# In the edge network of a graph kernel, the beginning of a chunk is put ahead of the network of the chunk in front of it

## The chip, the core and the metric

The kernel runs on one core of a Trainium2 chip. The time is the device time of one execution in microseconds (us), as the median of several runs. The profile is one further execution, recorded by the hardware profiler. The engines are named as in the profile: PE is TensorE (PEld its weight loads), DVE is VectorE, ACT is ScalarE, POOL is GpSimd and SP is SyncE. SP, ACT and POOL also issue DMAs; the gathers and scatters of single rows are all issued by POOL.

## What is computed

Four graph layers run one after the other over 6250 nodes of 48 features and 200000 edges, sorted by their end `dst`. The change touches the second layer only, a network on each edge whose results are averaged at the edge's end node:

```python
def _L1_gnn_ref(x, edge_index, edge_feat, W1, b1, W2, b2, W3, b3):
    source = edge_index[0]
    target = edge_index[1]
    edge = jnp.concatenate([x[source], x[target], edge_feat], axis=-1)   # 48 + 48 + 16
    h = jax.nn.relu(edge @ W1 + b1)                                       # 112 -> 128
    h = jax.nn.relu(h @ W2 + b2)                                          # 128 -> 128
    message = h @ W3 + b3                                                 # 128 -> 48
    msum = jax.ops.segment_sum(message, target, num_segments=n)
    cnt = jax.ops.segment_sum(jnp.ones(...), target, num_segments=n)
    return x + msum / jnp.maximum(cnt, 1.0)[:, None]
...
x = _layernorm(x + _L0_gnn_ref(...), axis=-1)
x = _layernorm(x + _L1_gnn_ref(x, edge_index, edge_attr_16, ...), axis=-1)
x = _layernorm(x + _L2_gnn_ref(x, edge_index, edge_weight), axis=-1)
x = _layernorm(x + _L3_gnn_ref(x, edge_index, 6250), axis=-1)
```

All matrices are 32-bit floats.

## The kernel before

Each of the 128 partitions holds a run of 1564 consecutive edges in sorted order, one edge per column. A loop over 41 chunks of columns (38 of 40 columns, then 24, 12 and 8) does the second layer in `edge_mlp`, lines 1172 to 1234. For one chunk `c` of the loop the program says, in this order:

- SP loads `r` (the edge's two ends, its weight and its 16 features, line 1181) and `q` (line 1183). In `q` a node's row stands only at the first edge of that node; elsewhere it is zero.
- `segments_chunk` (lines 801 to 803, DVE) writes the chunk's part of `other`, the indices for the gathers, and of `ns`, which is 1 where an edge has the same end as the one before it. ACT copies the weights into `dw` (line 1185).
- POOL gathers the row of the edge's other end from `tab_x` in device memory, one indirect DMA for each column (line 1188; in the profile line 166, the helper). They fill the first 48 of 112 numbers of an edge in the tile `t`.
- The rows of `q` are spread over the edges of a node by a scan along the columns (`runs`, lines 257 to 270). Four times, for 12 features each, ACT copies a part into PSUM (`run_v`, line 286), DVE adds what comes from the chunk before (line 267) and scans into `qf` (line 269). ACT copies `qf` into the next 48 numbers of `t` (line 1193) and the features from `r` into the last 16 (line 1194).
- The network goes over the chunk in turns of four columns: PE transposes four columns of `t` (line 1200), ACT copies them to `at` (1202), PE does the first layer (1207), ACT its relu to `h1` (1209), PE the second layer (1214), DVE its relu to `h2` (1216), PE the third layer (1222), and DVE copies the result to `msg` (1223). `skewed` puts the four stages of neighbouring turns side by side, so that turn i's transposes stand by turn i-1's first layer and so on.
- The messages are summed along the columns by another `runs` into `sf` (line 1227), copied to `st` by ACT (line 1230) and stored to `state_h` (line 1231). Later stages pick a node's sum out at its last edge.

The buffers come from pools: two of each tile in `ep` unless the call names another number. `qf`, `sf`, `msg` and `st` have one, `t`, `r`, `q`, `at`, `h1` and `h2` two. In PSUM the transposes, the first two layers together and the scans' `run_v` have two buffers each, and the third layer has one. A tile's buffer is free for the next tile of its name when the last reader of the old one is done. A planner puts every engine's instructions into one list, starting from the program's order but not bound to it; each engine then runs its list strictly in order, and waits where an instruction's operands or its buffer are not ready. So in the list of before a few small steps of later chunks, such as `other` and `ns`, already stand inside a chunk's network, while the scan of `q` and the copy into `t` stand behind the chunk before.

Of the kernel before, what the change touches and what calls it, by code (L numbers as in the profile page):

```python
# [20 lines left out]
N, E, H = 6250, 200000, 48  # L21
# [5 lines left out]
CHUNKS = [(i * C, C) for i in range(38)] + [(1520, 24), (1544, 12), (1556, 8)]  # L27
# [9 lines left out]
def pj(t):  # L37
    return t.rearrange("(p j) w -> p j w", j=J)
# [7 lines left out]
def gnn_kernel(ctx: ExitStack, tc: tile.TileContext, A, out: bass.AP):  # L46
    nc = tc.nc
    V, S, T = nc.vector, nc.scalar, nc.tensor
# [26 lines left out]
    before = const.tile([P, P], F32, name="before")  # L75
# [87 lines left out]
    tab_x = dram.tile([NP, H], F32, name="tab_x")  # L163

    def gather(dst, table, idx):
        return nc.gpsimd.indirect_dma_start(  # L166
            out=dst, out_offset=None, in_=table, in_offset=bass.IndirectOffsetOnAxis(ap=idx, axis=0))
# [37 lines left out]
    def by_columns(pool, wid, w, name, cols=C, **kw):  # L205

        return pool.tile([P, cols, w], F32, name=name, **kw)[:, :wid, :]

    def by_features(pool, w, wid, name, cols=C, **kw):

        t = pool.tile([P, w, cols], F32, name=name, **kw)
        return t.rearrange("p f c -> p (f c)")[:, :w * wid].rearrange("p (f c) -> p f c", c=wid)
# [28 lines left out]
    def factors(pool, name, fg=FG, cols=C):  # L241

        ts = [pool.tile([P, fg, cols], F32, name=f"{name}{i}", bufs=1) for i in range(2)]
        for t in ts:
            V.memset(t, 0.0)

        def put(c, v):
            wid = v.shape[1]
            t = ts[c % 2].rearrange("p f c -> p (f c)")[:, :fg * wid]
            u = t.rearrange("p (f c) -> p f c", c=wid)  # L250
            if wid < cols:
                V.memset(u[:, :, 0:1], 0.0)
            S.copy(u[:, :, 1:], v[:, None, 1:].to_broadcast([P, fg, wid - 1]))
            return t
        return put

    def runs(psum, dst, fac, first, before_, w, put, fg=FG, cols=C):


        wid = dst.shape[2]  # L260
        flat = dst.rearrange("p f c -> p (f c)")
        for f0 in range(0, w, fg):
            n = min(fg, w - f0)
            v = by_features(psum, fg, wid, "run_v", cols)
            put(v[:, :n, :], f0, n)
            if before_ is not None:
                V.scalar_tensor_tensor(v[:, :n, 0], before_[:, f0:f0 + n], first, v[:, :n, 0],  # L267
                                       op0=OP.mult, op1=OP.add)
            V.tensor_tensor_scan(flat[:, f0 * wid:(f0 + n) * wid], fac[:, :n * wid],  # L269
                                 v.rearrange("p f c -> p (f c)")[:, :n * wid], 0.0, OP.mult, OP.add)  # L270

    def kept_last(pool, t, name):

        k = pool.tile([P, t.shape[1]], F32, name=name)
        V.tensor_copy(k, t[:, :, t.shape[2] - 1])  # L275
        return k

    def by_feature(t):
        return t.rearrange("p c f -> p f c")

    def by_column(t):
        return t.rearrange("p f c -> p c f")

    def copied(src):

        return lambda v, f0, n: S.copy(v, by_feature(src[:, :, f0:f0 + n]))  # L286
# [504 lines left out]
    def segments_begin(k, pool):  # L791
        prev = pool.tile([P, 1], F32, name="seg_prev", bufs=1)
        V.memset(prev, -1.0)
        nc.sync.dma_start(prev[1:P, :], pj(rows[k][:])[0:P - 1, J - 1, 0:1])
        f = pool.tile([P, 1], F32, name="seg_first", bufs=1)
        nc.sync.dma_start(f, pj(rows[k][:])[:, 0, 0:1])
        V.tensor_copy(seg0, f)
        return prev, f

    def segments_chunk(j0, wid, r, prev):  # L800
        V.tensor_copy(other[:, j0:j0 + wid], r[:, :, 1])
        V.tensor_tensor(ns[:, j0:j0 + 1], r[:, 0, 0:1], prev, op=OP.is_equal)
        V.tensor_tensor(ns[:, j0 + 1:j0 + wid], r[:, 1:, 0], r[:, 0:wid - 1, 0], op=OP.is_equal)
        return r[:, wid - 1, 0:1]
# [23 lines left out]
    def skewed(n, *stages):  # L828

        kept = {}  # L830
        for i in range(n + len(stages) - 1):
            for k, stage in enumerate(stages):
                if 0 <= i - k < n:
                    kept[i - k] = stage(i - k, kept.get(i - k))
# [45 lines left out]
    def first_rows(pool, table, name):  # L880
        t = pool.tile([P, H], F32, name=name, bufs=1)
        gather(t, table[:], seg0[:, 0:1])
        return t
# [109 lines left out]
    with tc.tile_pool(name="e0", bufs=2) as ep:  # L993
        with tc.tile_pool(name="e0_ps", bufs=2, space=PSUM) as psum:
            f, last, sums = gated_sums(ep, psum)
# [176 lines left out]
    def edge_mlp(ep, psum, psum1, psum2):  # L1172
        W = 2 * H + EF
        prev, f = segments_begin("d", ep)
        factor = factors(ep, "fac")
        before_q = first_rows(ep, tab_x, "first")
        before_s = None
        for c, (c0, wid) in enumerate(CHUNKS):
            s = slice(c0, c0 + wid)
            r = by_columns(ep, wid, WD, "r")  # L1180
            nc.sync.dma_start(r, pj(rows["d"][:])[:, s, :])
            q = by_columns(ep, wid, H, "q")
            nc.sync.dma_start(q, pj(spread["d"][0:EP, :])[:, s, :])
            prev = segments_chunk(c0, wid, r, prev)
            S.copy(dw[:, s], r[:, :, 2])
            t = by_columns(ep, wid, W, "t")
            for j in range(wid):
                gather(t[:, j, 0:H], tab_x[:], other[:, c0 + j:c0 + j + 1])
            fac, first = factor(c, ns[:, s]), ns[:, c0:c0 + 1]
            qf = by_features(ep, H, wid, "qf", bufs=1)  # L1190
            runs(psum2, qf, fac, first, before_q, H, copied(q))
            before_q = kept_last(ep, qf, "last_q")
            S.copy(t[:, :, H:2 * H], by_column(qf))
            S.copy(t[:, :, 2 * H:], r[:, :, 3:])
            msg = by_columns(ep, wid, H, "msg", bufs=1)

            def turn(i, _):
                ps = psum.tile([W, 4, P], F32, name="ps_t")
                for k in range(4):
                    T.transpose(ps[:, k, :], t[:, 4 * i + k, :], ident)  # L1200
                at = ep.tile([W, 4, P], F32, name="at")
                S.copy(at, ps)
                return at

            def first_layer(i, at):
                ps = psum.tile([HID, 4, P], F32, name="ps_1")
                T.matmul(ps, w1, at, start=True, stop=True)  # L1207
                h1 = ep.tile([HID, 4, P], F32, name="h1")
                S.activation(h1, ps, AF.Relu, bias=b1)  # L1209
                return h1  # L1210

            def second_layer(i, h1):
                ps = psum.tile([HID, 4, P], F32, name="ps_1")
                T.matmul(ps, w2, h1, start=True, stop=True)  # L1214
                h2 = ep.tile([HID, 4, P], F32, name="h2")
                V.tensor_scalar(h2, ps, b2, 0.0, op0=OP.add, op1=OP.max)  # L1216
                return h2

            def third_layer(i, h2):
                ps = psum1.tile([P, 4, H], F32, name="ps_3")  # L1220
                for k in range(4):
                    T.matmul(ps[:, k, :], h2[:, k, :], w3, start=True, stop=True)  # L1222
                V.tensor_copy(msg[:, 4 * i:4 * i + 4, :], ps)

            skewed(wid // 4, turn, first_layer, second_layer, third_layer)
            sf = by_features(ep, H, wid, "sf", bufs=1)
            runs(psum2, sf, fac, first, before_s, H, copied(msg))
            before_s = kept_last(ep, sf, "last_s")
            st = by_columns(ep, wid, H, "st", bufs=1)
            S.copy(st, by_column(sf))  # L1230
            nc.scalar.dma_start(pj(state_h[0:EP, :])[:, s, :], st)
        lastf = ep.tile([P, 1], F32, name="lastf", bufs=1)
        V.tensor_copy(lastf, prev)
        return f, lastf, before_s

    with tc.tile_pool(name="e9", bufs=2) as ep:
        with tc.tile_pool(name="e9_ps", bufs=2, space=PSUM) as psum, \
                tc.tile_pool(name="e9_ps1", bufs=1, space=PSUM) as psum1, \
                tc.tile_pool(name="e9_ps2", bufs=2, space=PSUM) as psum2:
            f, lastf, sums = edge_mlp(ep, psum, psum1, psum2)  # L1240
        with tc.tile_pool(name="e9_ps3", bufs=1, space=PSUM) as psum:
            segments_end("d", ep, psum, f, lastf)
            carries(ep, psum, sums, H, 0)
# [112 lines left out]
```

## Time and profile before

| what | us |
|---|---|
| median of three runs | 21866.9 |
| lowest and highest of them | 21861.03, 21871.99 |
| the profiled execution | 21773.17 |
| its span, from the first to the last instruction | 21771.4 |
| busy: POOL, DVE, PE, ACT | 13854.5, 8090.9, 5782.7, 4790.3 |
| first gather of the second layer from `tab_x` (start) | 14080.9 |
| the second layer's last store, issued by ACT | 17144.5 |
| one gather from `tab_x`, busy, median | 0.944 |
| one copy of a whole chunk (`t<-qf` or `st<-sf`) | 3.917 |
| one `at` copy, one `h1`, one `h2`, one `msg` copy | 0.585, 0.688, 0.751, 0.358 |
| one scan of 480 columns, one `run_v` copy | 1.153, 0.97 |

The page gives one row for each group of instructions: line, engine, operation, output and inputs, how often, busy time and mean duration, and the idle time of the engine just before them with what ended most of it. A line can be that of a helper: all gathers have line 166 and all scans line 269. A timeline gives start, duration, engine, line and operation in order of time, with the idle time before the instruction in brackets and what ended it. In the trace the end of a matmul is modelled, and a few records of matmuls are missing. One matmul of 32-bit floats of the first or second layer shows as two records, so a turn has 16 of them: four transposes, two and two for the first layers, eight for the third.

### The profile page before, as it was taken

To read this page: it belongs to the slowest core of one execution; us is meant where nothing else is said; L and a number is where in the kernel's file an instruction comes from. 1 tells how busy PE (TensorE), PEld (TensorE's weight loads), DVE (VectorE), ACT (ScalarE), POOL (GpSimd) and SP (SyncE) were. 2 spreads that over 40 slices of the span, in tenths; PEclk is the share of its full clock that TensorE was granted. 3 is DMA by queue.
4 is the path that set the end of the run, shared out by engine and by line. 5 is a ranking of instruction groups with operands and counts; after the bars stand their busy time and mean duration, and the time that the engine had idled before them with its cause. 6 is when DMAs were issued, how large, how long until landed. Compare 5 with 4: busy or idle time off the path is not lost.

```text
span 21771.4 us, 87599 instructions
## 1 busy us (share of the span) xinstructions
PE 5782.7 (27%) x19726; PEld 3494.4 (16%) x19726; DVE 8090.9 (37%) x16421; ACT 4790.3 (22%) x6563; POOL 13854.5 (64%) x13410
## 2 busy tenths in 40 slices
PE   2332346622223222322223222245545200000000
PEld 2332334410002000200002000133333100000000
DVE  6554557644333344334333334322222211111001
ACT  0332334411111111111111111133333200001111
POOL 2666641177775777577775777644444577777777
PEclk9999995555555555555555555566666655555555
DMA  5455544332222222222222222211111111111111
GB/s 157 165 172 134 172 169 180 151 87 88 86 83 66 86 87 88 60 89 88 86 81 70 86 85 88 57 40 43 43 46 44 33 36 34 36 36 36 36 36 36
DMA packets 873560, 1792.36 MB, mean 82 GB/s; under 512 B 365490, under 2 KB 546658, under 8 KB 868034
## 3 DMA queue, kind: packets, MB, share of 16 engines
q1 hardware_dynamic: 349038, 860.63, 12.0%
q0 software_dynamic: 427520, 547.67, 10.8%
q10 hardware_dynamic: 96468, 378.32, 4.6%
q8 instruction: 167, 2.74, 0.1%
q14 instruction: 367, 3.01, 0.0%
HBM read 1144.48 MB, written 641.17 MB: 82 GB/s over the span
## 4 chain that ended last, share of the span: by engine, by line
POOL 43%; issue 21%; DVE 10%; another core or an unknown queue 10%; PE 9%; ACT 6%; DMA 1%; ACTq 0%; SPq 0%; POOLq 0%; DVEq 0%
POOL t L166 41%; PE ps L1207 2%; PE ps L1214 2%; PE ps L1222 1%; ACT run_v L286 1%; POOL own L166 1%; DVE qf L269 1%; DVE ol L303 1%; PE g L386 1%; DVE sf L986 1%; PE ps_t L1200 1%; ACT st L1230 1%; ACT st L989 1%; DVE run_v L267 1%
## 5 line engine op out<-in xcount | busy, mean ns | idle before, releaser
L166 POOL DMA_INDIRECT t<-tab_kv,other x6256 | 6576.9, 1051 | 2112.8 <-issue 2069.6
L166 POOL DMA_INDIRECT t<-tab_x,other x4692 | 4788.3, 1021 | 2605.8 <-issue 1457.2
L1124 PE MATMUL ka<-t,ident 128*128 128x480 f32 (+2 forms) x1264 | 1213.3, 1063 | 6798.6 <-DMA t<-tab_kv,other 6015.1
L1126 DVE TENSOR_TENSOR q<-qf,ka 128x480 f32<-128x480 f32 (+2 forms) x632 | 677.9, 1074 | 4126.9 <-issue 3358.9
L171 POOL DMA_INDIRECT rows_s<-r_s,scratch x1564 | 1527.9, 977 | 967.8 <-ACT r_s L421 466.7
L1124 PEld LDWEIGHTS ka<-t,ident 128*128 128x128 f32 x1264 | 316.3, 310 | 7520.9 <-issue 4273.1
L269 DVE TENSOR_TENSOR_SCAN qf<-fac,run_v 128x480 f32<-128x480 f32 (+1 forms) x943 | 1028.8, 1092 | 654.0 <-DVE run_v L267 409.8
L841 PE MATMUL cy_ps<-ident,last_s 128*48 128x128 f32 (+1 forms) x4 | 1.6, 406 | 4523.5 <-DVE last_s L275 4523.5
L1156 ACT COPY st<-m 128x40 f32<-128x40 f32 (+3 forms) x164 | 42.8, 261 | 5233.9 <-DVE sc L1129 4099.3
L386 PE MATMUL g<-hs,olt 128*128 128x49 f32 x3128 | 759.0, 418 | 1231.1 <-ACT hs L384 860.3
L286 ACT COPY run_v<-q 128x480 f32<-128x480 f32 (+1 forms) x943 | 851.7, 916 | 503.1 <-DVE qf L269 197.8
L1125 PE MATMUL ka<-r,tenth 128*128 128x400 f32 (+2 forms) x1264 | 959.7, 863 | 0.0
L1216 DVE TENSOR_SCALAR h<-ps,b 128x512 f32<-128x512 f32 x391 | 293.6, 751 | 1725.5 <-PE ps L1207 829.7
L386 PEld LDWEIGHTS g<-hs,olt 128*128 128x128 f32 x3128 | 696.1, 327 | 1283.6 <-ACT hs L384 893.0
L1304 DVE TENSOR_TENSOR run_v<-t,w_ps 128x480 f32<-128x480 f32 (+3 forms) x164 | 142.1, 912 | 1832.6 <-DMA t<-tab_x,other 1832.6
L267 DVE SCALAR_TENSOR_TENSOR run_v<-last_s,ns,run_v 128x12 f32<-128x12 f32 x480 | 98.0, 219 | 1934.1 <-issue 1280.6
L924 POOL TENSOR_TENSOR r<-r,u 128x1920 f32<-128x1920 f32 (+3 forms) x41 | 135.5, 3305 | 1034.3 <-DVE u L923 931.1
L269 DVE TENSOR_TENSOR_SCAN sf<-dec,run_v 128x480 f32<-128x480 f32 (+5 forms) x820 | 728.1, 921 | 36.1 <-remote 14.9
L841 PEld LDWEIGHTS cy_ps<-ident,last_s 128*48 128x48 f32 (+1 forms) x4 | 0.5, 126 | 4524.3 <-ACT st L1310 2261.5
L1207 PE MATMUL ps<-at,w 112*128 112x512 f32 x782 | 539.5, 779 | 506.8 <-ACT h L1209 428.3
L1155 ACT COPY st<-sf 128x1960 f32<-128x1960 f32 (+3 forms) x164 | 620.8, 3785 | 13.3 <-DVE run_v L267 11.0
L1148 DVE TENSOR_TENSOR run_v<-t,es 128x480 f32<-128x480 f32 (+2 forms) x656 | 616.1, 961 | 9.9 <-issue 5.1
(395 smaller groups left out, 15085.7 us busy)
## 6 DMA issues: line engine op xcount, KB each, us to landing
q<-spread_s SPq DMA_DIRECT2D x190, 960.0 KB
state_a<-st ACTq DMA_DIRECT2D x152, 1000.0 KB
r<-rows_a SPq DMA_DIRECT2D x152, 820.0 KB
state_h<-st ACTq DMA_DIRECT2D x114, 960.0 KB
t<-tab_kv,other POOLq DMA_INDIRECT x6256
r<-rows_s SPq DMA_DIRECT2D x38, 2480.0 KB
t<-tab_x,other POOLq DMA_INDIRECT x4692
seed<-zeros SPq DMA_DIRECT2D x17, 3726.0 KB
```

The costliest lines, as they stand in the source:

```text
L166: return nc.gpsimd.indirect_dma_start(out=dst, out_offset=None, in_=table, in_offset=bass.IndirectOffsetOnAxis(ap=idx, axis=0))
L171: i = nc.gpsimd.indirect_dma_start(out=table, out_offset=bass.IndirectOffsetOnAxis(ap=idx, axis=0), in_=src, in_offset=None)
L269: V.tensor_tensor_scan(flat[:, f0 * wid:(f0 + n) * wid], fac[:, :n * wid], v.rearrange("p f c -> p (f c)")[:, :n * wid], 0.0, OP.mult, OP.add)
L286: return lambda v, f0, n: S.copy(v, by_feature(src[:, :, f0:f0 + n]))
L386: T.matmul(g[:, b0 + b, :], olt[:, b0 + b, :], hs[:, b, :], start=True, stop=True)
L1124: T.matmul(ka, ident, t[:, j0:j1, 0:H], start=True, stop=False)
L1125: T.matmul(ka[:, :, 0:RBF], tenth, r[:, j0:j1, 0:RBF], start=False, stop=True)
L1126: V.tensor_mul(q[:, j0:j1, :], by_column(qf)[:, j0:j1, :], ka)
L1148: V.tensor_mul(v, by_feature(t[:, :, H + 1 + f0:H + 1 + f0 + n]), es[:, None, :].to_broadcast([P, n, wid]))
L1155: S.copy(st[:, :, 0:H + 1], by_column(sf))
L1207: T.matmul(ps, w1, at, start=True, stop=True)
L1214: T.matmul(ps, w2, h1, start=True, stop=True)
```

## The change

The first half of the loop's body, from the loads to the copies into `t`, becomes a function `begun(c)`. It is called once for chunk 0 ahead of the loop, and then in each pass for chunk c+1, ahead of the network of chunk c. What is carried from chunk to chunk is kept in a dictionary. The tile `t` has three buffers instead of two, `q` has one instead of two, and the two scans' outputs `qf` and `sf` share one tile name, `scanned`, with one buffer between them. The instructions of the network, the sums and the stores are as they were.

```diff
-        before_q = first_rows(ep, tab_x, "first")
-        before_s = None
-        for c, (c0, wid) in enumerate(CHUNKS):
+        before = {"q": first_rows(ep, tab_x, "first"), "s": None, "prev": prev}
+
+        def begun(c):
+
+            c0, wid = CHUNKS[c]
             s = slice(c0, c0 + wid)
             r = by_columns(ep, wid, WD, "r")
             nc.sync.dma_start(r, pj(rows["d"][:])[:, s, :])
-            q = by_columns(ep, wid, H, "q")
+            q = by_columns(ep, wid, H, "q", bufs=1)
             nc.sync.dma_start(q, pj(spread["d"][0:EP, :])[:, s, :])
-            prev = segments_chunk(c0, wid, r, prev)
+            before["prev"] = segments_chunk(c0, wid, r, before["prev"])
             S.copy(dw[:, s], r[:, :, 2])
-            t = by_columns(ep, wid, W, "t")
+            t = by_columns(ep, wid, W, "t", bufs=3)
             for j in range(wid):
                 gather(t[:, j, 0:H], tab_x[:], other[:, c0 + j:c0 + j + 1])
             fac, first = factor(c, ns[:, s]), ns[:, c0:c0 + 1]
-            qf = by_features(ep, H, wid, "qf", bufs=1)
-            runs(psum2, qf, fac, first, before_q, H, copied(q))
-            before_q = kept_last(ep, qf, "last_q")
+            qf = by_features(ep, H, wid, "scanned", bufs=1)
+            runs(psum2, qf, fac, first, before["q"], H, copied(q))
+            before["q"] = kept_last(ep, qf, "last_q")
             S.copy(t[:, :, H:2 * H], by_column(qf))
             S.copy(t[:, :, 2 * H:], r[:, :, 3:])
+            return t, fac, first
+
+        ahead = begun(0)
+        for c, (c0, wid) in enumerate(CHUNKS):
+            s = slice(c0, c0 + wid)
+            t, fac, first = ahead
+            if c + 1 < len(CHUNKS):
+                ahead = begun(c + 1)
             msg = by_columns(ep, wid, H, "msg", bufs=1)
...
             skewed(wid // 4, turn, first_layer, second_layer, third_layer)
-            sf = by_features(ep, H, wid, "sf", bufs=1)
-            runs(psum2, sf, fac, first, before_s, H, copied(msg))
-            before_s = kept_last(ep, sf, "last_s")
+            sf = by_features(ep, H, wid, "scanned", bufs=1)
+            runs(psum2, sf, fac, first, before["s"], H, copied(msg))
+            before["s"] = kept_last(ep, sf, "last_s")
             st = by_columns(ep, wid, H, "st", bufs=1)
             S.copy(st, by_column(sf))
             nc.scalar.dma_start(pj(state_h[0:EP, :])[:, s, :], st)
...
-        V.tensor_copy(lastf, prev)
-        return f, lastf, before_s
+        V.tensor_copy(lastf, before["prev"])
+        return f, lastf, before["s"]
```

In the planned lists of the changed kernel, PE has the first two turns' transposes of chunk c+1 ahead of the last third layer of chunk c. In ACT's list, behind the third `h1` of a network, stand a `run_v` copy of `q`, the `st` copy of the chunk before, `fac` and further `run_v` copies of `q`, then `at` and `h1` of the next turns, and behind the fifth `h1` the copy of the scanned rows into `t` of the chunk after. In DVE's list the scans of the chunk after stand between the third and the fourth `h2`. POOL's list of gathers is in the same order as before.

## The prediction

> **What bounds the kernel now.** I read the page's 40 slices first: the stage that the diff touches is where PEclk shows sixes. The times of the gathers from `tab_x` place it at 14080.9 to 17147 us of the span, 3066 us. The busy time of that stretch comes next: POOL 1477, PE 1515, ACT 1147, DVE 870 us. No engine is busy for half of it, so waits set the time. The waits from 14300 to 17100 (columns: total us, times, longest us):
>
> ```profile
> POOL t L166 <- ACT at L1202: 1017.2, 37, 30.2
> DVE h L1216 <- PE ps L1207: 826.8, 60, 27.6
> PE ps_t L1200 <- ACT t L1193: 640.3, 29, 23.1
> ACT at L1202 <- remote: 419.4, 60, 9.4
> ```
>
> The gathers wait for the network's transposes to free a buffer of `t`, the transposes wait for the copy of the scanned rows into `t`, and something called "remote" holds the network. One chunk's timeline (start, duration, engine, idle before and its end) shows how these meet:
>
> ```profile
> 15012.40 3.92 ACT L1193 COPY t<-qf 128x1920 f32<-128x1920 f32 x1 [1.09 <-DVE qf L269]
> 15016.37 1.96 PE L1200 MATMUL ps_t<-ident,t 128*112 128x128 f32 x8 [22.39 <-ACT t L1193]
> ...
> 15022.28 0.60 PE L1200 MATMUL ps_t<-ident,t 128*112 128x128 f32 x4
> ...
> 15030.43 0.59 ACT L1202 COPY at<-ps_t 112x512 f32<-112x512 f32 x1 [9.17 <-remote]
> ...
> 15034.12 0.94 POOL L166 DMA_INDIRECT t<-tab_x,other  x1 [0.30 <-issue]
> 15035.98 0.69 ACT L1209 ACTIVATE h<-ps,b 128x512 f32<-128x512 f32 x1 [4.96 <-remote]
> ...
> 15041.70 0.58 ACT L1202 COPY at<-ps_t 112x512 f32<-112x512 f32 x1 [5.04 <-remote]
> ...
> 15062.01 0.94 POOL L166 DMA_INDIRECT t<-tab_x,other  x1 [26.95 <-ACT at L1202]
> ```
>
> Up to 15062.0 the trace holds 520 gathers of chunks (13 chunks) and 480 transposes (12 chunks). So the network that starts at 15016.4 is that of the twelfth chunk, and the gathers beside it fill the thirteenth: gathers already run ahead. The cycle is: last transpose, 40 gathers of 1.248 us (50 us), 27 us of POOL idle until the next network's last transpose; 36 such cycles take 16993.7 - 14211.6 = 2782 us, **77.3 us each**.
>
> Between 15022.9 and 15041.7 the network stands still although PE had issued its next transposes. The first chunk, whose network lies beside two chunks of gathers (14080.9 to 14180.4), shows the same for 80 us; a late chunk, whose gathers end at 17023.4, just as its network starts, does not show it at all:
>
> ```profile
> 14109.82 0.58 ACT L1202 COPY at<-ps_t 112x512 f32<-112x512 f32 x1 [9.17 <-issue]
> 14115.38 0.69 ACT L1209 ACTIVATE h<-ps,b 128x512 f32<-128x512 f32 x1 [4.97 <-remote]
> 14132.22 0.59 ACT L1202 COPY at<-ps_t 112x512 f32<-112x512 f32 x1 [16.16 <-remote]
> 14137.78 0.69 ACT L1209 ACTIVATE h<-ps,b 128x512 f32<-128x512 f32 x1 [4.97 <-remote]
> 14177.02 0.58 ACT L1202 COPY at<-ps_t 112x512 f32<-112x512 f32 x1 [38.56 <-remote]
> ...
> 17035.69 0.58 ACT L1202 COPY at<-ps_t 112x512 f32<-112x512 f32 x1 [1.50 <-PE ps_t L1200]
> 17036.49 0.69 ACT L1209 ACTIVATE h<-ps,b 128x512 f32<-128x512 f32 x1 [0.22 <-PE ps L1207]
> 17038.68 0.58 ACT L1202 COPY at<-ps_t 112x512 f32<-112x512 f32 x1 [1.50 <-PE ps_t L1200]
> ```
>
> Without gathers a turn (four columns through the three layers, 16 matmul records) takes 2.99 us. Beside gathers ACT sees a two-matmul layer 5.56 us after its predecessor, and a full turn takes 44.8 us (14132.22 to 14177.02): 2.8 us a matmul. About ten matmuls after an idle PE still arrive in time. The delay ends 7.6 us after the last gather (15034.1 to 15041.7). The trace does not name the cause; the coincidence with gathers holds in every chunk that I looked at.
>
> **The change, part by part.** *Same work.* Gathers, scans, copies and matmuls stay 1:1 (PE's list of instructions grows by 38 rows because runs of transposes are split). Nothing is saved but waiting.
>
> *The serial stretch.* From a network's last transposes (15060.7) to the next network's first (15093.6) PE now waits 33 us: tail of the network (to 15074), scan of its sums, `st` copy, the next rows' scan, the 3.92 us copy into `t`. In the new order the first transposes of the next chunk stand on PE ahead of the last third layer, with copies and scan done a chunk earlier. So the next network starts about 29 us earlier, some 6 us after the gathers restart instead of 31.6.
>
> *What is late next.* That gain lands inside the gathers. They need 50 us as before, since the third buffer only makes more full buffers wait: each network still empties one, and only then does POOL fill it. From 15062 on, the tail still runs nearly freely for about 9 us (its last third layer arrives some 3 us late, 12.0 us after the restart). From +9 to the release at +57.6 us the price of 2.8 us allows 48.6 / 2.8 = 17 matmuls. Before, the new network needed 24 matmuls to reach the point it has at the release (8 for two transposes, 2+4+2+2+4+2): ten free, the rest in the 22 us left or in the release. After, 8 transposes are done by +9 and 17 more follow: 25, **the same point**. The bounds: if ten free ones also come, 10 x 0.19 us = 1.9 us a chunk is won; if the last third layer (8 matmuls) falls under the price too, up to one turn, 3 us, is lost. I take 0.
>
> *What is moved into the network.* ACT's list after the third `h1` now holds one copy of `q` (0.97), the `st` copy (3.92), `fac` (0.58), three more copies of `q` (2.9) and the copy into `t` (3.92): 12.3 us, which lay in the 33 us gap. Behind them, in order, wait `at` and `h1` of turns 4 and 5, and so PE. The third `h1` comes with the release, so this falls into the fast part. The third copy of `q` also waits for DVE's first scan, which stands behind the third `h2`, and the fourth `h2` stands behind all four scans. After the release six turns are left, 19.7 us before (15041.7 to 15061.4). ACT has 2.99 - 1.27 = 1.72 us to spare in each: over six turns 10.3 us, so at least 2.0 us is not covered; over the first three, where the work stands, 5.2 us, so at most 7.1. The copies hold up the front turns, yet part of the pause is caught up by the double buffers: **+4.5 us**, the middle. If it fell into the slow window, it would cost nothing.
>
> *Loads and small parts.* `r` and `q` are the same DMAs, up to two chunks further ahead on SP. `q` with one buffer waits for the four copies a chunk earlier, and has over 40 us to land; the first-chunk wait of 17.1 us for it is the only one in the trace: 0. The shared `scanned` tile makes the next rows' scan wait for the `st` copy and the sums' scan for the `t` copy; ACT's order has both in between: in the 4.5.
>
> *Start and end.* Three chunks are gathered at once: the first network leaves the slow window 50 us later. In return one full cycle fewer follows, and the last four small chunks have no 33 us gaps. The end costs 77.3 + 54.6 + 41.4 + 57.4 = 230.7 us before (the last full cycle, then to 17048.3, 17089.7, 17147); estimated from 24, 12 and 8 gathers, 7.6 us release and the turns, 62 + 46 + 32 + 32 = 172 after. Together 50 + 172 - 230.7 = -9.
>
> **Sum:** 35 x 4.5 - 9 = +149 us on the execution's own 21773.2 (span 21771.4), 21922. The median of the runs is 21866.9, 93.7 above that; with it **22015 us**.
>
> **The rule that speaks against this sum.** The Trainium skill, "SBUF — State Buffer", section "Who interferes with whom", says that "DMA never contends with a compute engine". By it the network beside gathers would take its 30 us, and POOL would never stop: 1564 x 1.248 = 1952, and some 60 for the last chunks' networks, 2012 us for the stage, 1054 less: 20813. The rows above disagree: 44.8 us a turn beside gathers and 2.99 without. The page speaks of SBUF's ports; what the delay is here is open, but I follow the row.
>
> **Rivals.** *A, full overlap (20813):* the slow state may need a PE that starts cold from idle. For it: at the restart of the gathers a running PE loses only 3 us in 12. Against: the first network stays slow for 80 us whatever PE does, and the late chunk also starts from idle without it. 0.12. *B, a small gain:* ten free matmuls and the copies inside the slow window: 35 x -1.9 - 9 = -76, 21791. For: ten come free at each start now. 0.14. *C, nothing moves:* POOL still waits for one network per chunk, and copies are caught up; 21867. 0.10. *D, the main forecast, slower through ACT's copies:* 0.48. *E, slower through PE:* transposes and the last third layer share the priced window; from ten priced matmuls more on, one turn is missing at the release: 3 + 4.5 to 7.1, taken as 9 us a chunk, +306, 22173. For: third layers beside gathers took 22 us in the first chunk. 0.16.
>
> **Numbers.** Slower by over 0.2% (44 us; about what a measurement can tell from none): D and E, 0.64; within: 0.10; faster: A and B, 0.26. Range: low end 21720 (B with a little more), high end 22330 (E with the 7.1 and a turn: 10.1 x 35 = 354, and 100 for the start); A and rare worse cases stay outside. D's own range is 21920 to 22120.
>
> **What would show it.** Right: gathers of a chunk start every 80 to 84 us; POOL's wait before them stays near 30 us and names `at`; "remote" waits of ACT at `at` and `h1` grow; PE no longer waits 22 us for the copy into `t`; ACT's `st` and `t` copies stand between `at` copies of one network. Wrong: a POOL without pauses (A); `at` copies 3 us apart beside gathers, which would break the price of 2.8 us; a period below 77 us with the third `h1` well before the last gather (B).

## The result and the profile after

| | before | changed |
|---|---|---|
| median of four runs, us | 21869.44 | 21988.88 |
| lowest and highest | 21861.03, 21872.61 | 21980.84, 22010.71 |
| span of the profiled execution | 21771.4 | 21985.9 |
| first gather of the stage to the first of the next stage | 3154.3 | 3284.2 |
| from one chunk's first gather to the next one's, mean of 32 | 77.3 | 81.1 |
| POOL's pause in it | 27.6 | 31.4 |

The changed kernel is slower: ratio 1.0055, 95% interval 1.0043 to 1.0067. The two profiled executions are further apart (214.5 us) than the medians (119). Of that, 83.4 us lie ahead of the stage's first gather (14080.9 and 14164.3 us), 129.9 in the stage, 1.2 behind it. The first part is not the change's: another execution of the kernel before, recorded later, has its first gather at 14166.3.

These are the waits of the changed kernel from 14300 to 17100 us (columns: total us, times, longest us), to be read beside those of the kernel before:

```profile
POOL t L166 <- ACT at L1212: 1068.2, 34, 33.5
ACT at L1212 <- remote: 788.8, 86, 38.6
DVE h L1226 <- remote: 512.6, 55, 24.2
...
ACT h L1219 <- remote: 271.1, 87, 10.6
```

PE's 640 us of waiting for the copy into `t` are gone, so the serial stretch is removed as intended. POOL's wait for `at` did not go with it, it grew (34 waits of 31.4 us where there were 37 of 27.5), and ACT's "remote" waits before `at` grew from 419 to 789 us. ACT's timeline for one network shows where the pause comes from (start, duration, engine, idle before and its end). POOL had issued the last gather at 15045.1 and starts the next one at 15077.9:

```profile
15050.65 0.58 ACT L1212 COPY at<-ps_t 112x512 f32<-112x512 f32 x1 [13.15 <-remote]
15052.79 0.69 ACT L1219 ACTIVATE h<-ps,b 128x512 f32<-128x512 f32 x1 [1.56 <-remote]
...
15054.25 3.92 ACT L1240 COPY st<-scanned 128x1920 f32<-128x1920 f32 x1
...
15060.78 0.58 ACT L1212 COPY at<-ps_t 112x512 f32<-112x512 f32 x1
...
15066.48 3.92 ACT L1195 COPY t<-scanned 128x1920 f32<-128x1920 f32 x1 [0.49 <-DVE scanned L269]
15070.31 0.58 ACT L1212 COPY at<-ps_t 112x512 f32<-112x512 f32 x1
...
15077.24 0.58 ACT L1212 COPY at<-ps_t 112x512 f32<-112x512 f32 x1 [1.50 <-PE ps_t L1210]
```

The line at 15050.65 is the fourth `at` of ten, the last `at` that comes late; the third `h1` at 15052.79 is the last late result of all, 56.4 us after the chunk's first gather (14996.41). From the fourth `at` to the tenth it takes 26.6 us, where the kernel before took 19.7 (15041.70 to 15061.36). The 10.1 us between the fourth and the fifth hold the `st` copy, the next interval but one (5.5 us) the copy into `t`, both with hardly a wait beside them: ACT works nearly straight through.

Over the 5th to the 36th chunk the means are (us):

| | fourth `at`, from the first gather | fourth to tenth `at` | third `h1`, from the first gather | third `h1` to tenth `at` | tenth `at`, from the first gather |
|---|---|---|---|---|---|
| before | 56.3 | 20.4 | 56.8 | 19.9 | 76.7 |
| changed | 53.1 | 27.4 | 55.8 | 24.6 | 80.4 |

To the last column, 0.6 us are missing to the period. The late results end at the same place in both: the last ACT or DVE instruction that waits for one starts 56.3 us (before) and 56.4 us (changed) after the chunk's first gather, by the median. In the kernel before the fourth `at` stands at that end. In the changed kernel it is usually let through some 3 us earlier, and the third `h1` stands at the end. So the third `h1` tells better than the fourth `at` what is won beside the gathers and what is lost behind: the network is 1.0 us further on when the late results end, and 4.8 us slower from there.

### The profile page after: what moved, and what is told of

The parts are those of the page before. It is cut to its first block, busy times and chain, and to the rows that moved or that the text cites. A ratio compares the mean times of both kernels' runs of the same rounds, so it can differ in the third digit from the quotient of the medians.

```text
span 21985.9 us, 87626 instructions
## 1 busy us (share of the span) xinstructions
PE 5966.8 (27%) x19726; PEld 3527.6 (16%) x19726; DVE 8077.6 (37%) x16421; ACT 4752.4 (22%) x6563; POOL 13874.4 (63%) x13410
## 4 chain that ended last, share of the span: by engine, by line
POOL 42%; issue 21%; another core or an unknown queue 12%; DVE 10%; PE 8%; ACT 5%; DMA 1%; ACTq 0%; SPq 0%; POOLq 0%; DVEq 0%
POOL t L166 40%; ACT run_v L286 2%; PE ps L1232 1%; PE ps L1217 1%; POOL own L166 1%; PE ps L1224 1%; DVE ol L303 1%; PE g L386 1%; DVE qf L269 1%; DVE sf L986 1%; PE ps L973 1%; ACT st L1240 1%; PE ps_t L1210 1%; ACT st L989 1%
## 5 line engine op out<-in xcount | busy, mean ns | idle before, releaser
L269 DVE TENSOR_TENSOR_SCAN qf<-fac,run_v 128x480 f32<-128x480 f32 (+4 forms) x779 | 847.6, 1089 | 644.3 <-DVE run_v L267 382.2
L1224 PE MATMUL ps<-h,w 128*128 128x512 f32 x782 | 547.1, 789 | 515.3 <-ACT h L1219 350.9
```

## The experiments

**Two sorts of chips.** The runs came from several chips, and these are of two sorts. On some the kernel before takes 21761 to 21886 us, as in the runs above; on others 18722 to 18731. On the second sort no result of PE comes late. I call them chips with and without late results. Every ratio is to the kernel before on the same chip, and stretches in us are compared within one sort.

**e1 and s1: the two long copies on DVE.**

```diff
-            S.copy(t[:, :, H:2 * H], by_column(qf))
+            V.tensor_copy(t[:, :, H:2 * H], by_column(qf))
...
-            S.copy(st, by_column(sf))
+            V.tensor_copy(st, by_column(sf))
```

> The changed kernel with its two 3.92 us copies (scanned rows into t, sums into st) on DVE instead of ACT; the lists of PE, ACT and DVE are otherwise the same. Theory D (the 3.8 us a chunk come from ACT's copies in the fast part): ACT's share there falls from 12.3 to 4.5 us, below the 5.2 us it has to spare, and DVE, with 1.1 us of each 2.99 us turn, hides its own; the period falls from 81.1 to about 77, the stretch from the fourth at copy to the tenth from 26.6 to about 20, the time to about 21845 us (21800 to 21890). Theory E (the loss comes from PE's results shown late beside the gathers): the stretch stays near 26, the period at 81, the time at 21989 within 44.

On a chip without late results it took 18717.37 us, ratio 0.9993 (0.9984 to 1.0002). Neither theory of the expectation could be tested there. The same kernel once more:

> The changed kernel with its two 3.92 us copies on DVE, once more, for a chip with the late results (before at some 21870; the run before was on a chip without them, where the copies on DVE made a gather take 1.326 instead of 1.248 us). There: theory D: period from 81.1 to about 77, but with 40 gathers slowed a little beside DVE's copies; fourth to tenth at copy from 26.6 to 20 to 22 us; time 21850 to 21900. Theory E: stretch near 26, time at 21989 within 44. On the other chip again: 18717.

With late results: 21744.79 us beside 21764.93, ratio 0.9991 (0.9983 to 1.0). Period 76.8, stage 3116.9 us. Theory E would have left 81. The stretch from the fourth to the tenth `at` did not shrink as expected (26.2 us), but the fourth `at` now comes 50.0 us after the first gather, while results are still late. From the third `h1` (54.9 us) to the tenth `at` it takes 21.3 us, where the changed kernel needs 24.6. The sum, and with it the period, fell by 4.3 us a chunk. In its trace both copies (2.03 us each on DVE, at 15083.3 and 15094.0) lie behind the gathers of a chunk (15026.3 to 15076.0), in POOL's pause.

**e2 and s2: the copies stay on ACT, but ahead of the network.** The first `h1` and the third `at` are held behind the copy into `t` on ACT.

```diff
+            tail["copied"] = S.copy(t[:, :, H:2 * H], by_column(qf)).ins
...
-                S.copy(at, ps)
+                with tc.issue_after(tail["copied"]) if i == 2 else ExitStack():
+                    S.copy(at, ps)
...
-                S.activation(h1, ps, AF.Relu, bias=b1)
+                with tc.issue_after(tail["copied"]) if i == 0 else ExitStack():
+                    S.activation(h1, ps, AF.Relu, bias=b1)
```

> The changed kernel with its first h1 and third at copy held on ACT behind the copy of the scanned rows into t, so that all of the tail (st, fac, the scan of q, the copy into t) stands in ACT's list between the second at copy and the first h1, beside the gathers. Theory D: the 12.3 us lie where ACT waits for PE's late results anyway; the fast part is back at some 20 to 22 us and the period at 76 to 78.5, the time at 21800 to 21900. Theory E: what counts is the number of matmuls shown by the release; with h1 held up fewer are, so the period stays at 81 or grows to 84, the time 21989 to 22100.

Again a chip without late results: 18645.56 us, ratio 0.9954 (0.9937 to 0.997). Once more:

> The tail of the chunk in front held ahead of the first h1 and the third at copy, once more, for a chip with the late results. Theory D: fast part of 20 to 22 us, period 76 to 78.5, time 21800 to 21900. Theory E: fewer matmuls shown by the release since h1 is held up: period 81 to 84, time 21989 to 22100. On the other chip again: 18646.

With late results: 21747.31 us, ratio 0.9994 (0.9985 to 1.0003), period 76.1. In ACT's timeline the two copies (at 15054.4 and 15064.0) now lie beside the gathers, which run from 15027.9 to 15077.6.

Two quite different edits, which both take the two copies (7.84 us) out of ACT's list behind the late results, give back 4.3 and 5.0 us a chunk (s2 moves the small parts of the tail with them). The loss is ACT's copies, as theory D had it. Here too the fourth-to-tenth stretch missed the 20 to 22 us expected (27.5), with the fourth `at` at 48.0; from the third `h1` (54.6) it is 20.9. s2 is not clearly better than s1 in time, although its period is: from the first gather of the 39th chunk to the next stage it takes 283 us, s1 248 and the kernel before 241.

**e3 and e4: the order alone and the buffers alone.** e3 keeps the new order and goes back to two buffers of `t`, two of `q` and a tile each for `qf` and `sf`. e4 is the kernel before with the new buffers. For e3:

```diff
-            q = by_columns(ep, wid, H, "q", bufs=1)
+            q = by_columns(ep, wid, H, "q")
-            t = by_columns(ep, wid, W, "t", bufs=3)
+            t = by_columns(ep, wid, W, "t")
-            qf = by_features(ep, H, wid, "scanned", bufs=1)
+            qf = by_features(ep, H, wid, "qf", bufs=1)
...
-            sf = by_features(ep, H, wid, "scanned", bufs=1)
+            sf = by_features(ep, H, wid, "sf", bufs=1)
```

> The new order alone: t with two buffers, q with two, qf and sf each a tile of their own, as before. The forecast took the third buffer and the shared tile as free: period 81 as in the changed kernel, only the start differs (two chunks gathered at once, -27 to +30 us): 21950 to 22020. Rival: the buffers carry the loss (the shared tile's waits, or three chunks gathered at once): near the kernel before, 21869 within 44, or clearly below 21950.

> The buffers alone in the old order: t with three, q with one, qf and sf sharing one tile. Forecast: each network still empties one buffer, so the period stays at 77.3 and the start and end move the time by -50 to +50: 21820 to 21920. Rival: waits on the shared tile (the scan of q behind the st copy) lie in the serial stretch and lengthen it by up to 3.9 us a chunk; if the start of the network set the period, 21869 + 141 = 22010.

Both ran without late results: e3 18599.44 us, ratio 0.9929 (0.9913 to 0.9946); e4 18742.56, ratio 1.0005 (0.9997 to 1.0014). These expectations were written for the other sort, so they are neither met nor missed. What the traces show is the stage that I had priced as the rival of full overlap. ACT's timeline of e4 beside gathers:

```profile
13402.57 0.59 ACT L1202 COPY at<-ps_t 112x512 f32<-112x512 f32 x1 [1.50 <-PE ps_t L1200]
13403.38 0.69 ACT L1209 ACTIVATE h<-ps,b 128x512 f32<-128x512 f32 x1 [0.22 <-PE ps L1207]
13405.57 0.59 ACT L1202 COPY at<-ps_t 112x512 f32<-112x512 f32 x1 [1.50 <-PE ps_t L1200]
```

A turn takes 3.0 us with gathers running, and a gather starts every 1.248 us without a pause. In the old order (e4) the network's own cycle is some 53.5 us, longer than the 49.9 of its gathers; it falls behind, the gathers wait for it from the 34th chunk on, and the stage takes 2209 us. In the new order (e3) POOL never waits for it and the stage takes 2061. So without late results the order is worth 131 us against the kernel before. Against e4 the stage is 148 us shorter, 129 of them behind the first gather of the 39th chunk. The new buffers without the order bring nothing there. Neither kernel was tried on a chip with late results.

**r1 and r2: both kernels once more.**

> The changed kernel once more, since the four runs before ran on a chip on which the kernel before takes 18731 us and the gathers beside the networks run without a pause. Theory 'the late results decide': on a chip that shows the kernel before at some 18731, the changed kernel has no late results and no pauses of POOL either, gathers every 1.248 us, and is faster than before by 90 to 150 us as the new order alone was (131): 18580 to 18640. On a chip with the late results (before at some 21870) it is slower by 0.4 to 0.7%, with a period of 81. Rival 'the copies on ACT decide everywhere': slower than before by some 100 us on either chip.

> The kernel before once more, for its trace on this chip. On a chip with before at 18731: gathers every 1.248 us for most of the stage, POOL's pauses few and under 5 us until the last four small chunks, ACT's at copies 3 us apart beside gathers, the stage some 2210 us from first gather to the next stage's. On a chip with before at 21870: period 77.3 again, results late by 2.8 us a matmul, the stage 3156 us, and the stages ahead of it as long as in the run that was shown or up to 96 us longer, which would tell where the 96 us between the profiled execution and the median lie.

They ran with late results, and slower by 0.5% as expected there. Changed: 21989.15 us beside 21886.09, ratio 1.005 (1.0034 to 1.0067), period 81.2, stage 3290. Before: period 77.3, stage 3159, first gather at 14166.3; of the 91 us by which this execution (21864.22) is longer than the profiled one shown above, 85 lie ahead of the stage. Whether the changed kernel is faster than before on the other sort of chip was not tried; e3 makes it likely.

**p1 to p4: a little work between the gathers.** The two sorts of chips also differ in long runs of gathers. These lines are for the gathers of the next stage, which wait for no other engine (times, minimum, median and maximum in ns, first and last start). First before, with late results, then e4, without:

```profile
L166 POOL DMA_INDIRECT t<-tab_x,other x1512: 940/949/1936, 17300.1 to 19396.7; - x189
```

```profile
L166 POOL DMA_INDIRECT t<-tab_x,other x1523: 940/944/966, 14700.1 to 16599.9; - x191
```

POOL issues one every 1.248 us on both, but on the first chip only for the first 190 or so; then single gathers take up to 1.94 us to issue, and the rate settles at 1.4005 us each (mean of the 400th to the 1500th). All eight traces with late results show this rate there, and all six without show 1.248. It looks as if on the first sort each gather leaves something behind that is worked off more slowly than POOL issues, so that a backlog grows.

It is not the rows themselves that lag. In the chunk of the prediction's timeline the last gather starts at 15034.12 and results are late until 15041.70. What the queues moved from 15034 to 15044, in 40 slices of 0.25 us, is over by 15036.25 (the two gathers have 32 packets each):

```profile
GB/s 0 0 98 0 0 0 0 86 12 0 0 0 0 0 0 0 0 0 0 0 0 0 0 0 0 0 0 0 0 0 0 0 0 0 0 0 0 0 0 0
DMA packets 64, 0.05 MB, mean 5 GB/s; under 512 B 32, under 2 KB 64, under 8 KB 64
```

In the next stage DVE has the rows of the 160th gather in a row 2.6 us after that gather starts, as it had those of the 40th:

```profile
17433.62 0.94 POOL L166 DMA_INDIRECT t<-tab_x,other  x1 [0.30 <-issue]
...
17436.23 1.82 DVE L1304 TENSOR_TENSOR run_v<-t,w_ps 128x480 f32<-128x480 f32 x2 [41.29 <-DMA t<-tab_x,other]
```

What the backlog consists of stays open. But the late results follow it: in ACT's timeline of the changed kernel they last well past the last gather issued for the first network, which started at 14312.9:

```profile
14304.92 0.58 ACT L1212 COPY at<-ps_t 112x512 f32<-112x512 f32 x1 [38.56 <-remote]
...
14337.19 0.59 ACT L1212 COPY at<-ps_t 112x512 f32<-112x512 f32 x1 [25.34 <-PE ps_t L1210]
```

From the start of the last of 40, 80 and 120 gathers in a row to the end of the late results it takes 7.6, 17.3 and 24.3 us (before; first chunk of before; this one). Counted from the first gather it is 56.3, 115.9 and 172.9 us: 1.41, 1.45 and 1.44 us for each gather, close to the 1.4005 of the long run. If the backlog is the cause, gathers issued at a slower pace than it is worked off must run beside a network that is not held up. So a fill on POOL was put behind each gather:

```diff
+        pause = ep.tile([P, 320], F32, name="pause", bufs=1)
...
-                gather(t[:, j, 0:H], tab_x[:], other[:, c0 + j:c0 + j + 1])
+                tc.keep_in_program_order(gather(t[:, j, 0:H], tab_x[:], other[:, c0 + j:c0 + j + 1]))
+                tc.keep_in_program_order(nc.gpsimd.memset(pause, 0.0))
```

First with 128 columns, in the changed kernel and in the one before:

> The changed kernel with a fill of a 128x128 tile on POOL behind each of these gathers (0.2 us by the row of the same fill at the start of the kernel), so that a gather starts every 1.45 to 1.55 us instead of 1.248. Theory Q (the results are late while gathers stand in a queue behind POOL: where before takes some 21800, long runs of gathers settle at 1.4005 us each, so 40 that are issued in 50 us are through at 56.0, and the fourth at copy comes 56.3 us after the first): paced slower than 1.40, nothing queues, no result is late, the network of 30 to 50 us lies wholly beside the gathers, POOL hardly pauses, period 58 to 63, time some 39 x 19 = 740 us below the changed kernel: 21050 to 21350. Rival R (results are late whenever gathers are under way): the gathers take 60 us, the late window grows with them, period 81 + 8 to 10, time 22300 to 22400. On a chip where before takes 18731 gathers are the bound and both say 18600 + 39 x 10 = 19000.

> The kernel before with the same fills. Theory Q: no late results; its own cycle without them was 53.5 us on the other chip, below the 58 to 63 us of the paced gathers, so it is as fast as the changed kernel paced, within 60 us: 21050 to 21400. Then the order of the chunks is worth nothing either way once the gathers are paced, but for the start and end. Rival R: 77.3 + 10, time 22150 to 22260. On a chip with before at 18731: 19050 to 19150.

No late results on this chip, so these runs tell nothing of the cause: 18727.34 us, ratio 1.0003 (0.9994 to 1.0012), and 18746.14, ratio 1.0013 (1.0006 to 1.002). They show the pace: 1.335 us, too little, since the fill of 0.22 us partly replaces idle time. With 320 columns:

> The changed kernel with a wider fill (128x320) behind each gather: the fill of 128x128 made a gather start every 1.335 us, which is still below the 1.4005 us at which long runs of gathers settle where before takes some 21800; one of 320 should make it 1.48 to 1.56. Theory Q (results are late while gathers stand in a queue behind POOL; in the traces of before and of the changed kernel the late results end 7.6, 15.5 and 22.6 us after the last of 40, 80 and 120 gathers was issued, as for a queue that takes some 1.4 us each): nothing queues, no late results, POOL hardly pauses, period 59 to 63, time 21100 to 21400 on a chip where before takes some 21800. Rival R (late whenever gathers are under way): period 88 to 92, 22250 to 22450. On a chip where before takes 18731 the gathers alone bind: 38 x 60 + 80 = 2360 for the stage, some 19000.

(The delays named there were read a little differently; the 7.6, 17.3 and 24.3 above are all from the start of the last gather.) This chip had late results: **21066.63 us beside 21774.71, ratio 0.9677 (0.9661 to 0.9693)**. That is a little below the range expected. The period is 60.0 us, POOL's longest idle time 0.9, the stage 2452 us. The waits from 14300 to 16400 and two lines of POOL's timeline:

```profile
DVE h L1229 <- PE ps L1227: 913.0, 324, 8.2
...
POOL t L166 <- issue: 230.1, 1382, 0.9
```

```profile
15000.49 0.38 POOL L1193 MEMSET pause<- 128x320 f32 x1
15001.04 0.95 POOL L166 DMA_INDIRECT t<-tab_x,other  x1 [0.17 <-issue]
```

Slower gathers, one every 1.50 us instead of 1.248, and a faster kernel: POOL's wait for `at`, over 1000 us before, is gone from the list, and so is every "remote" wait of ACT and DVE. Rival R, lateness with any gather under way, would have made it slower. That it is the pace, and not merely another instruction between two gathers, is argued and not shown: the smaller fill, at 1.335 us still below 1.4005, would have told, but p1 and p2 had no late results to remove. The last run asks whether the order matters then:

> The kernel before with the 128x320 fill behind each gather, beside the changed kernel with it (21067, ratio 0.9677, on a chip where before takes 21775). Theory Q: no late results; the old order's own cycle without them was 53.5 us, below the 60 us of the paced gathers; as fast as the changed kernel paced but for the start and end, and slower by up to 150 us there (the last four small chunks with their 27 to 39 us pauses): ratio 0.968 to 0.976. Rival S (the pacing helps only with the new order, since in the old one the network still stands behind the serial stretch): POOL pauses in each chunk, ratio 0.98 to 1.0. On a chip where before takes 18731: 1.02 to 1.03.

21085.78 us beside 21760.72, ratio 0.969 (0.9674 to 0.9706), on a chip of the sort with late results by its time for the kernel before and by the 1.4005 us of its next stage. The period is again 60.0, the stage 2469 us. Rival S falls: the intervals of p3 and p4 overlap, and the stages differ by 17 us, all of it at the end.

## Why the prediction was right

- **The bound** was read rightly: POOL waits for one network per chunk, and the network stands still beside gathers. PE's 22 us waits for the copy into `t` went, POOL's pause stayed near 30 us (31.4), still naming `at`, "remote" waits grew, and the `st` and `t` copies stand between `at` copies: each sign that I had named.
- **"The gain lands inside the gathers", 0 us, between -1.9 and +3 a chunk.** The mechanism was right: although the network's first `at` comes 9.3 us after the first gather instead of 32.0, its third `h1` comes with the end of the late results, 55.8 us after the first gather where it was 56.8. The gain is 1.0 us, within the bound of 1.9 for the ten free matmuls.
- **Copies moved into the network, +4.5 us a chunk, between 2.0 and 7.1.** From the third `h1` to the tenth `at` it takes 4.8 us more (19.88 to 24.64), and taking the copies away gave 4.3 (s1) and 5.0 (s2) back. Together it is 3.8 us a chunk, where +4.5 was forecast. The 4.5 was only the middle of its bounds, so that it is so close is in part luck. s2 also bears out that the copies cost nothing in the slow window.
- **Rival E** (PE's priced window, +9) falls with s1 and s2.
- **Start and end, -9 us.** The 35 chunks from the 4th to the 39th took 132.2 us longer, the start 25.1 less, the end 22.9 more: -2. Cut at the same places, the forecast's parts are 50 - 77.3 = -27 for the start and 172 - 153.4 = +19 for the end. The sum of +149 was 130.
- **Profile and median.** I added the whole 93.7 us between them. That was right for the median: most of it lies ahead of the stage (85 us of 91 in r2), and the changed execution agrees with its own median within 1.2 us. The forecast of 22015 is 26 us above the median; on the move it is 146 forecast against 119.
- **The rule weighed against the row.** I followed the row, 44.8 us a turn beside gathers against 2.99, and set aside "DMA never contends with a compute engine" (Trainium skill, "SBUF — State Buffer", "Who interferes with whom"). For the forecast that was right. But "beside gathers" was too wide a reading of the row: p3 and p4 have gathers beside the network all the time and no late result, and on the other chips no result is late either. The runs fit a price that holds only where gathers are issued faster than their backlog is worked off. I had noted that the late results end 7.6 us behind the last gather and not asked why 7.6: it is 40 gathers at 0.15 to 0.2 us of lag each, 0.15 being 1.4005 - 1.248.
- **Rival A** was priced for a cause that this change does not touch. Its stage of 2012 us is close to what e3 had without late results (2061).

Open: what the backlog is, since the rows land in time, and why it holds up PE's results at all. The price of 2.8 us a matmul is twice the 1.4005 us of a gather, which suggests that each result waits for two of them; no run tests it. Why the chips differ is open too.

## What to carry to other kernels

Before a stage is reordered to overlap two things, find out what happens while they already overlap: here the overlap itself was the slow part, and moving work into it or out of it changed the time by half a per cent, while issuing the gathers a fifth slower took three per cent off, in either order. Where an engine issues many small transfers, measure the rate of a long run against that of a short one, and look at how long a delay lasts past the last issue: a backlog can show there although every transfer lands in time. What is moved off a serial stretch still needs its engine's time, so ask where in that engine's list it lands, and whether that engine has room there.

## What the runs showed of the hardware

- The same kernel takes 18.7 thousand us on some chips and 21.8 on others. The sustained gather rate differs (1.248 and 1.4005 us), and the stage took 3154 us on one sort and 2209 with the new buffers on the other, with the old order on both.
- On the slower sort back-to-back gathers leave what looks like a backlog. It shows in PE's results and, after some 190 gathers, in POOL's issue. It does not show in the data: the last gather's packets end some 2 us after its start.
- A copy on DVE stretches a gather's issue. In e1 each long copy meets the gathers, and two of 40 took 2.2 to 2.8 us instead of 0.94, so a chunk's gathers took 53.0 us instead of 49.9:

```profile
13402.75 2.02 DVE L1195 COPY t<-scanned 128x1920 f32<-128x1920 f32 x1
...
13403.05 2.55 POOL L166 DMA_INDIRECT t<-tab_x,other  x1 [0.30 <-issue]
```

  The gather ends 0.83 us after the copy (13405.60 and 13404.77), as if it had waited for it. The same section of the Trainium skill's "SBUF — State Buffer" says that a DVE copy in a mode that uses both its ports keeps GpSimd from writing a DMA's descriptors; the trace agrees, but does not show in which mode the copy ran. It is why e1 gains nothing there although e3 gains 0.7%: 38 chunks at 3.05 us make up the 115 us between their stages. In s1 the copies fell into POOL's pause and held up no gather.
- A fill of 0.22 us between two gathers delays the next by only 0.087 us (1.248 to 1.335), one of 0.38 us by 0.25.
